# A graph network's start: edges and x transferred before W, packed edges written from another queue, scores chained tile by tile

## The chip, the cores and the metric

The kernel runs on one core of one Trainium2 chip. The metric is the device time of one execution in microseconds (us). A core has five engines that run side by side and meet through semaphores: TensorE (PE in the profile; its weight loads are PEld), VectorE (DVE), ScalarE (ACT), GpSimd (POOL) and SyncE (SP). SP, ACT and POOL can issue DMA transfers, each on a queue of its own (SPq, ACTq, POOLq); the transfers run on 16 DMA engines of the core.

## The reference, cut to what matters

625 nodes with rows x of 1024 values, 20000 edges (`src`, `dst`, a type from 0 to 7). Layer 0 is a graph attention, layer 1 a relational convolution with a gate; each is added to its input and normalised.

```python
h = x @ W                                    # 625 x 1024
al = h @ a_l ; ar = h @ a_r
e = exp(-leaky_relu(al[src] + ar[dst], 0.1)) # one score per edge
rowsum = segment_sum(e, src)
h_prime = segment_sum(e[:, None] * h[dst], src) / (rowsum[:, None] + EPS)
x = layernorm(x + elu(h_prime))
# layer 1
u = x @ root + bias
for r in range(8):                           # mean over the incoming edges of type r
    u = u + mean_r(x) @ weight[r]
z = concat([u, x], 1) @ w_gate + b_gate
x = layernorm(x + tanh(u) * z + x * (1 - z))
```

## The kernel before, in words

The function `fast` does the work. (A second function, `general`, is only entered when the edge counts show that `fast` lost an edge.) Nodes are cut into five tiles of 125 rows.

Layer 0 never gathers rows by edge. It counts how often each pair (source, destination) occurs, by type, and works with dense 625 x 625 matrices:

- *Edges.* The lists dst, src and type are loaded as 125 rows of 160 (L700) into a part of the buffer of `attT`; x's first tile is loaded between the first and the second (L702). These four loads are issued from ACT's queue. W comes in eight chunks of 128 rows from SP's queue (`load_w0`, L567), then x's second tile (L706) and the two halves of `a` (L707, L708). POOL writes two small pads around the DRAM tensor `packed` (L704, L705).
- *Packing.* VectorE converts the lists and packs each edge into one number (L721, L727 to L731). ACT's queue writes the result to `packed` in DRAM (L733). VectorE also compares samples of the sorted list with the first row of each group of destinations (`less`, L723).
- *Groups.* TensorE sums `less` into the place where each group's edges begin (p_count, L737, L738). VectorE turns this into block numbers (L740, L742), and POOL gathers those blocks from `packed` by two indirect DMAs (L746).
- *h's first tile.* `x_turned` transposes x's tile on TensorE (L673) and copies it with ScalarE (L714). `h_parts` multiplies it by W chunk by chunk, two matmuls of 512 columns for each of eight chunks (L779); each float32 matmul shows as two records of the trace. Before the last chunk, `place_edges` turns the gathered edges with TensorE (p_edges, L753) and VectorE splits them into sources and keys (L756 to L764).
- *Counting.* For each of 55 groups VectorE builds one-hot matrices (`one_hots`, L805), and TensorE multiplies them (`counts_of`, L829); ScalarE copies the counts out (L834). In between, TensorE computes the other four tiles of h. `row_sums` (L790) forms al and ar, `all_types` (L842 to L846) adds the types into one count `c` per pair, and the counts go to DRAM for layer 1 (`store_counts`, L881).
- *Scores.* `scores_of(j)` forms the scores `e` of one tile of destinations j against all five tiles of sources (L859 add, L862 multiply by the count cut at 1, L863 leaky relu, L864 exponential on ScalarE, L865 multiply by the count, L866 reduce to `rsum`). `turn_scores(j)` transposes them (patt, L875) and ScalarE copies them to `attT` (L877). `gather_h(t, j)` multiplies them with h (phh, L684).
- *After that.* `attend(t)` divides, applies the elu and normalises (L1058 to L1068), and layer 1's matrix products follow (L1015, L1016, L1019, L1185). Their weights are split on ScalarE and VectorE into three pieces (`prepare`, L988 to L991); the first of these splits, of `root`, lie already beside the scores.

The order of the score work is written with a list `due`: while the groups are counted, a piece of work is done when its group number comes. `AHEAD` tiles of scores are put on that list (L927), the others are computed in the loop of gathers:

```python
        turn_scores(0, es[0])
        for j in range(ST):
            gather_h(0, j)
            if len(es) < ST:
                es.append(scores_of(len(es)))
            if j + 1 < ST:
                turn_scores(j + 1, es[j + 1])
            for t in range(1, EARLY):
                gather_h(t, j)
```

This is the order of the source. A scheduler then fixes the order of the instructions on each engine, and it moves instructions that do not depend on each other past one another. On an engine they run strictly in that fixed order. Each DMA signals its landing on a semaphore; the DMAs of SP and ACT take eight of these in turn, so that a DMA waits until the one eight places before it has landed.

Of the kernel before, what the change touches and what calls it, by code (L numbers as in the profile page):

```python
# [10 lines left out]
F32 = mybir.dt.float32  # L11
F16 = mybir.dt.float16
BF16 = mybir.dt.bfloat16
I32 = mybir.dt.int32
I16 = mybir.dt.int16
AF = mybir.ActivationFunctionType
OP = mybir.AluOpType
# [423 lines left out]
ST = 5  # L441
TN = N // ST
SP = ST * 128
BLOCK = 32
NBLOCK = E // BLOCK
GCOLS = 12
NG = -(-TN // GCOLS)
NGS = ST * NG
# [4 lines left out]
HOTS = 5  # L453
H_GROUPS = 38
LAG = 4
AHEAD = 3
EARLY = 3
MAGIC = 1.5 * 2.0 ** 23
EPS12 = 2.0 ** -12
# [32 lines left out]
def rows_of(t):  # L492
    return TN
# [30 lines left out]
def fast(  # L524
# [16 lines left out]
    nc = tc.nc  # L541
# [13 lines left out]
    def bank(name):  # L555
        return ps[0].tile([128, 512], F32, tag="bank", name=name)


    def load_w0(wpool):

        chunks = []
        for k in range(KC):
            if k % 2:
                w = rawp.tile([128, 2, HALF], F32, tag="raw", name=f"w0_{k}").rearrange("p i c -> p (i c)")
            else:
                w = wpool.tile([128, D], F32, tag="w", name=f"w0_{k}")
            nc.sync.dma_start(w, w0[k * 128:(k + 1) * 128, :])  # L567
            chunks.append(w)
        return chunks
# [18 lines left out]
    ones16 = const.tile([128, 1], F16, name="ones16")  # L588
# [5 lines left out]
    ahead16 = const.tile([1, NGS, 2], F16, name="ahead16")  # L594
    nc.gpsimd.iota(ahead16, pattern=[[0, NGS], [128 // BLOCK, 2]], base=0, channel_multiplier=0,
                   allow_small_or_imprecise_dtypes=True)
    later = const.tile([128, 2, 4], F32, name="later")
# [15 lines left out]
    rsum = const.tile([128, ST, ST], F32, name="rsum")  # L613
# [29 lines left out]
    packed = dram.tile([NBLOCK + 5, BLOCK], F32, name="packed")  # L643
# [4 lines left out]
    def move_rows(n, dma):  # L648

        r0 = 0  # L650
        for m in (n // 16 * 16, n % 16):
            dma(slice(r0, r0 + m))
            r0 += m

    def load_x(pool, t, name, bufs=None, eng=nc.sync, clear=False):

        xt = pool.tile([128, D], F32, tag="x", name=f"{name}_{t}", bufs=bufs)
        if t < ST - 1:
            eng.dma_start(xt, x[t * TN:t * TN + 128, :])
        else:  # L660
            if clear:
                nc.gpsimd.memset(xt[96:], 0.0)
            xr = x[t * TN:t * TN + rows_of(t), :]
            move_rows(rows_of(t), lambda rows: eng.dma_start(xt[rows], xr[rows]))
        return xt
# [22 lines left out]
    with tc.tile_pool(name="f_w", bufs=4, side="right") as wpool, \  # L688
# [7 lines left out]
        per = E // TN  # L696
        edge_rows = free[:TN, D:D + 3 * per].bitcast(I32).rearrange("p (i c) -> p i c", i=3)
        rest, pack, samples = (free[:TN, D + i * per:D + (i + 1) * per] for i in (3, 4, 5))
        for i, ap in ((1, dst), (0, src), (2, etype)):
            nc.scalar.dma_start(edge_rows[:, i, :], ap.rearrange("(p c) -> p c", c=per))  # L700
            if i == 1:
                x_next = load_x(xin, 0, "x", eng=nc.scalar)  # L702
        w0_sb = load_w0(wpool)
        nc.gpsimd.dma_start(packed[0:1, :], pad[:, :BLOCK])  # L704
        nc.gpsimd.dma_start(packed[NBLOCK + 1:, :].rearrange("(o i) c -> o (i c)", o=1), pad)  # L705
        x_next = [x_next, load_x(xin, 1, "x")]  # L706
# [3 lines left out]
        def x_turned(t):  # L710
            n = rows_of(t)
            xt = x_next.pop(0)
            xT = xin.tile([128, KC, 128], F32, tag="xT", name=f"xT_{t}")
            transposed(xt, n, f"px_{t}", lambda ks, p: nc.scalar.copy(xT[:, ks, :n], p))  # L714
            if t + 2 < ST:
                x_next.append(load_x(xin, t + 2, "x"))
            return xT
# [4 lines left out]
        less = scores.tile([TN, per // BLOCK, 2 * NGS], F16, name="less")  # L722
# [7 lines left out]
        nc.vector.scalar_tensor_tensor(pack, edge_rows[:, 1, :], float(LO * TR), pack, op0=OP.mult, op1=OP.add)  # L730
        nc.vector.scalar_tensor_tensor(pack, edge_rows[:, 2, :], float(LO), pack, op0=OP.mult, op1=OP.add)  # L731
        packed_rows = packed[1:NBLOCK + 1, :].rearrange("(p m) c -> p (m c)", p=TN)
        nc.scalar.dma_start(packed_rows, pack)  # L733
        xT_next = x_turned(0)
        p = bank("p_count")
        for m in range(per // BLOCK):
            nc.tensor.matmul(p[:2 * NGS, :1], less[:, m, :], ones16[:TN], start=m == 0, stop=False)  # L737
        nc.tensor.matmul(p[:2 * NGS, :1], ahead16.rearrange("p g h -> p (g h)"), ones16[:1], start=False, stop=True)  # L738
        base = scores.tile([2 * NGS, 1], F32, name="base")
        nc.vector.tensor_copy(base, p[:2 * NGS, :1])  # L740
        at_block = scores.tile([2 * NGS, 2, 4], I32, name="at_block")
        nc.vector.tensor_scalar(at_block, later[:2 * NGS], base, float(NBLOCK + 1), op0=OP.add, op1=OP.min)  # L742
        edges = scores.tile([2 * NGS, 2, 4, BLOCK], F32, name="edges")
        for b in range(2):

            nc.gpsimd.indirect_dma_start(edges[:, b].rearrange("p i c -> p (i c)"), None, packed[:, :],  # L746
                                         bass.IndirectOffsetOnAxis(ap=at_block[:, b, :1], axis=0))

        def place_edges():

            pe = bank("p_edges")[:, :4 * NGS]
            for b in range(2):
                nc.tensor.transpose(pe[:, b * 2 * NGS:(b + 1) * 2 * NGS], edges[:, b].rearrange("p i c -> p (i c)"),  # L753
                                    ident[:2 * NGS, :2 * NGS])
            q = scores.tile([128, 4 * NGS], F32, name="q")
            nc.vector.tensor_scalar(q, pe, 1.0 / LO, 0.5 / LO - 0.5, op0=OP.mult, op1=OP.add)  # L756
            nc.vector.tensor_scalar(q, q, MAGIC, MAGIC, op0=OP.add, op1=OP.subtract)

            def twice(ap):
                return ap.unsqueeze(2).to_broadcast([128, 4 * NGS, 2])  # L760

            nc.vector.tensor_tensor(key2.rearrange("p b g h w -> p (b g h) w"), twice(q),
                                    twice(firsts.rearrange("p b g h -> p (b g h)")), op=OP.subtract)
            nc.vector.scalar_tensor_tensor(src2.rearrange("p b g h w -> p (b g h) w"), twice(q), -float(LO), twice(pe),  # L764
                                           op0=OP.mult, op1=OP.add)
# [8 lines left out]
        def h_parts(t, xT):  # L774
            n = rows_of(t)
            halves_h = [ps_h.tile([128, 512], F32, tag="ph", name=f"ph_{t}_{half}") for half in range(2)]
            for k in range(KC):
                for half, p in enumerate(halves_h):
                    nc.tensor.matmul(p[:n, :], xT[:, k, :n], w0_sb[k][:, half * HALF:(half + 1) * HALF],  # L779
                                     start=k == 0, stop=k == KC - 1)  # L780
                if k == KC - 1:
                    for half, p in enumerate(halves_h):
                        nc.scalar.copy(h_sb[:n, t, half * HALF:(half + 1) * HALF], p[:n, :])
                yield
# [64 lines left out]

        ar_b = attp.tile([128, SP], F32, name="ar_b")  # L850

        def scores_of(j):

            n = rows_of(j)
            cols = slice(j * 128, j * 128 + n)
            c1 = ct[j]
            e = attp.tile([128, ST, 128], F32, name=f"e_{j}")
            e = e[:, :, :n]
            nc.vector.tensor_tensor(e, ar_b[:, cols].unsqueeze(1).to_broadcast([128, ST, n]),  # L859
                                    al.unsqueeze(2).to_broadcast([128, ST, n]), op=OP.add)  # L860

            nc.vector.scalar_tensor_tensor(e, c1, 1.0, e, op0=OP.min, op1=OP.mult)  # L862
            nc.vector.scalar_tensor_tensor(e, e, SLOPE, e, op0=OP.mult, op1=OP.max)  # L863
            nc.scalar.activation(e, e, AF.Exp, scale=-1.0)  # L864
            nc.vector.tensor_tensor(e, e, c1, op=OP.mult)  # L865
            nc.vector.tensor_reduce(rsum[:, :, j], e, axis=AX.X, op=OP.add)  # L866
            return e

        def turn_scores(j, e):
# [11 lines left out]
                nc.sync.dma_start(cd[r][:, :, j * 128:(j + 1) * 128], cj[:, :, r, :])  # L881

        for k, _ in enumerate(h_parts(0, xT_next)):
            if k == KC - 2:
                place_edges()
        due = [(LAG, row_sums, 0)]
# [32 lines left out]
        for i in range(NGS):  # L919
            while steps < min(n_steps, (i + 1) * n_steps // H_GROUPS):  # L920
                next(h_steps, None)
                steps += 1
                if steps % KC == 0:
                    due.append((i + (LAG if steps < n_steps else 0), row_sums, steps // KC))
                    if steps == n_steps:
                        due.append((i + 6, lambda _: spread_ar(), None))
                        due.extend((max(i + 6 + 4 * j, (j + 1) * NG + LAG), lambda _: es.append(scores_of(len(es))), None)  # L927
                                   for j in range(AHEAD))
            if i % NG == 0:
# [20 lines left out]
# [8 lines that stand above are left out]
# [169 lines left out]
    p = bank("p_ins")  # L1127
# [8 lines left out]
    p = bank("p_all")  # L1136
# [22 lines left out]
    for r in range(R):  # L1159
        for h in range(2):  # L1160
# [13 lines left out]
            c = cf[0]  # L1174
# [119 lines left out]
```

## Time and profile before

| | us |
|---|---|
| median of 3 runs (lowest to highest) | 979.65 (977.29 to 980.05) |
| the profiled execution's own time | 980.44 |
| its span, first to last instruction | 978.5 |
| TensorE busy | 945.4 |
| VectorE busy | 595.6 |
| ScalarE busy | 391.3 |
| GpSimd busy | 38.4 |

The profile is of one execution. "Busy" is the time in which an engine ran an instruction; the rest of the span it waited, and the profile says for what, with the line of the kernel. A line such as `PE px L673 <- DMA x<-in_x_dram` reads: TensorE, at the transposes of line 673 that write px, waited for the DMA that writes x. Tables of stretches give for each stretch the busy time of each engine and the number of its instructions, then the clock granted to TensorE (1.00 is full), the busy share of the DMA engines and the bytes they moved.

### The profile page before, as it was taken

Reading aid. Unit: us, or ns where it says so; the run is one execution under the profiler, and the core shown is the slowest. Engines: PE = TensorE matmul, PEld = TensorE weight load, DVE = VectorE, ACT = ScalarE, POOL = GpSimd, SP = SyncE. Lnnn points to the kernel's source line nnn. Section 1 sums busy time; section 2 is a strip of 40 time slices with the busy share of each in tenths; the row PEclk is TensorE's granted clock in tenths of the full one; section 3 lists DMA queues with packets and bytes.
Section 4 is the critical chain, followed back from the end, with each engine's and each line's share of the span. In section 5 each row is a group of like instructions: output and inputs, shape, how many; then the busy total and the mean of one; then the engine's idle time right before and its main releaser. Section 6 shows DMA issues by size and latency. Waiting matters only on the chain.

```text
span 978.5 us, 10845 instructions
## 1 busy us (share of the span) xinstructions
PE 945.4 (97%) x4075; PEld 731.2 (75%) x4075; DVE 595.6 (61%) x955; ACT 391.3 (40%) x714; POOL 38.4 (4%) x68
## 2 busy tenths in 40 slices
PE   3999899999999999999999999999999999999995
PEld 1455554878888888888888888888888888888874
DVE  1697898986536456266365463562653644639995
ACT  0233656344515515425435345244442551433422
POOL 2000001000000000000000000000000000002123
PEclk9999989999999999999999999999999999999998
DMA  7132773533213022122121220320320211432213
GB/s 273 45 76 54 194 203 108 173 117 112 64 34 116 26 65 76 45 86 66 55 86 44 77 87 10 110 65 22 120 65 22 86 37 49 143 114 66 86 43 108
DMA packets 61713, 83.89 MB, mean 86 GB/s; under 512 B 29311, under 2 KB 29833, under 8 KB 61654
## 3 DMA queue, kind: packets, MB, share of 16 engines
q1 hardware_dynamic: 60830, 82.17, 27.1%
q10 hardware_dynamic: 664, 0.84, 0.3%
q8 instruction: 34, 0.56, 0.2%
q14 instruction: 25, 0.20, 0.1%
q0 software_dynamic: 160, 0.11, 0.0%
HBM read 71.36 MB, written 11.75 MB: 85 GB/s over the span
## 4 chain that ended last, share of the span: by engine, by line
PE 94%; DVE 2%; DMA 1%; ACT 1%; issue 0%; POOL 0%; ACTq 0%; POOLq 0%; DVEq 0%
PE pu L1185 19%; PE p_w L1015 15%; PE p_w L1016 15%; PE p_w L1019 15%; PE ph L779 7%; PE phh L684 5%; PE p_root L1019 2%; PE p_root L1015 2%; PE p_wgx L1019 2%; PE p_wgx L1016 2%; PE p_wgx L1015 2%; PE p_root L1016 2%; PE pc L829 2%; DMA attT<-in_edge_type_dram 1%; PE p_wgu L1019 1%; PE p_wgu L1016 1%
## 5 line engine op out<-in xcount | busy, mean ns | idle before, releaser
L1016 PE MATMUL p_w<-m_w,x_l 128*128 128x512 f32 x640 | 249.1, 389 | 0.0
L1015 PE MATMUL p_w<-g_w,x_h 128*128 128x512 f32 x640 | 249.0, 389 | 0.0
L1185 PE MATMUL pu<-y,cf 125*128 125x512 f32 x800 | 184.4, 389 | 0.0
L1167 DVE SCALAR_TENSOR_TENSOR v<-p_w,v 125x512 f32<-125x512 f32 x80 | 55.2, 690 | 201.8 <-PE p_w L1019 153.0
L1019 PE MATMUL p_w<-e_w,x_d 128*128 128x512 f32 x640 | 176.4, 389 | 0.0
L1185 PEld LDWEIGHTS pu<-y,cf 125*128 125x128 f32 x800 | 150.2, 188 | 31.5
L1019 PEld LDWEIGHTS p_w<-e_w,x_d 128*128 128x128 f32 x640 | 120.2, 188 | 25.5 <-DVE e_w L991 0.3
L1016 PEld LDWEIGHTS p_w<-m_w,x_l 128*128 128x128 f32 x640 | 120.2, 188 | 25.1 <-DVE m_w L990 0.2
L1015 PEld LDWEIGHTS p_w<-g_w,x_h 128*128 128x128 f32 x640 | 120.2, 188 | 25.0
L1166 ACT ACTIVATE v<-p_w 125x512 f32<-125x512 f32 x80 | 47.6, 596 | 214.0 <-PE p_w L1016 214.0
L990 DVE SCALAR_TENSOR_TENSOR m_w<-raw_w,e_w 128x512 fp32r<-128x512 f32 x128 | 84.7, 682 | 36.4 <-ACT e_w L989 36.4
L1170 DVE TENSOR_TENSOR y<-v,y 125x512 fp32r<-125x512 f32 x80 | 55.2, 690 | 50.8 <-ACT y L1169 50.8
L988 ACT ACTIVATE g_w<-raw_w 128x512 fp32r<-128x512 f32 x128 | 73.2, 621 | 29.8 <-PE p_w L1015 20.7
L991 DVE TENSOR_TENSOR e_w<-g_w,m_w 128x512 fp32r<-128x512 f32 x128 | 84.7, 682 | 0.5
L1169 ACT CAST y<-v 125x512 fp32r<-125x512 f32 x80 | 49.2, 615 | 75.1 <-DVE v L1167 75.1
L779 PE MATMUL ph<-w,xT 128*125 128x512 f32 x160 | 77.7, 614 | 1.1 <-ACT xT L714 1.1
L989 ACT ACTIVATE e_w<-raw_w 128x512 fp32r<-128x512 f32 x128 | 73.2, 623 | 0.0
L1189 DVE SCALAR_TENSOR_TENSOR L_gnn_bias_dram_u<-pu,inv,L_gnn_bias_dram_u 125x512 f32<-125x512 f32 x80 | 55.4, 740 | 0.5
L1151 ACT CAST cf<-cs 128x640 fp32r<-128x640 f16 x40 | 25.9, 724 | 54.7 <-PE pu L1185 46.1
L779 PEld LDWEIGHTS ph<-w,xT 128*125 128x125 f32 x160 | 27.9, 192 | 25.0 <-issue 22.3
L1232 POOL TENSOR_TENSOR L_gnn_bias_dram_u<-L_gnn_bias_dram_u,xr 125x512 f32<-125x512 f32 x10 | 17.0, 1697 | 744.5 <-ACT L_gnn_bias_dram_u L1217 711.9
L684 PE MATMUL phh<-h_sb,attT 125*125 125x512 f32 x100 | 45.8, 613 | 0.2 <-ACT attT L877 0.2
(156 smaller groups left out, 969.5 us busy)
## 6 DMA issues: line engine op xcount, KB each, us to landing
raw_w<-in_L_gnn_weight_dram SPq DMA_DIRECT2D x64, 512.0 KB
cd<-cj SPq DMA_DIRECT2D x40, 160.0 KB
cs<-cd SPq DMA_DIRECT2D x8, 800.0 KB
w<-in_L_gnn_W_dram SPq DMA_DIRECT2D x8, 512.0 KB
raw_root<-in_L_gnn_root_dram SPq DMA_DIRECT2D x8, 512.0 KB
raw_wgx<-in_L_gnn_w_gate_dram SPq DMA_DIRECT2D x8, 512.0 KB
raw_wgu<-in_L_gnn_w_gate_dram SPq DMA_DIRECT2D x8, 512.0 KB
x<-in_x_dram SPq DMA_DIRECT2D x7, 512.0 KB
```

The lines of the kernel that those rows point to most:

```text
L684: nc.tensor.matmul(banks_h[t, half][:n, :], attT[:nj, j, tile_cols(t)], h_sb[:nj, j, half * HALF:(half + 1) * HALF], start=(j == 0), stop= ...
L779: nc.tensor.matmul(p[:n, :], xT[:, k, :n], w0_sb[k][:, half * HALF:(half + 1) * HALF], start=k == 0, stop=k == KC - 1)
L988: nc.scalar.activation(g, w, AF.Copy, scale=DOWN)
L989: nc.scalar.activation(e, w, AF.Copy, scale=UP12 * DOWN)
L990: nc.vector.scalar_tensor_tensor(m, w, UP12, e.bitcast(F32), op0=OP.mult, op1=OP.subtract)
L991: nc.vector.tensor_tensor(e, g.bitcast(F32), m.bitcast(F32), op=OP.subtract)
L1015: nc.tensor.matmul(p1, h[:, k, :], g, start=k == 0, stop=False, skip_group_check=True)
L1016: nc.tensor.matmul(p1, l[:, k, :], m, start=False, stop=k == KC - 1, skip_group_check=True)
L1019: nc.tensor.matmul(p2, d[:, k, :], e, start=k == 0, stop=k == KC - 1, skip_group_check=True)
L1167: nc.vector.scalar_tensor_tensor(v[:n], p2, -EPS12, v[:n], op0=OP.mult, op1=OP.add)
L1185: nc.tensor.matmul(p, c[:m, t, j * 128:(j + 1) * 128], piece[:m], start=(t == 0 and i == 0), stop=(t == ST - 1 and i == 1), skip_group_che ...
L1189: nc.vector.scalar_tensor_tensor(at, p[:n], inv[:n, j, r:r + 1], at, op0=OP.mult, op1=OP.add)
```

## The change

Four edits. The three edge lists and x's first tile are loaded from SP's queue, ahead of W, and no longer from ACT's. The packed edges are written from POOL's queue. The group counts with what follows them, up to the gathers, become a function that is called after the first step of h's first tile. The scores of a tile depend on the sum of the tile before: the scalar 1.0 of the multiply is read from a column of a new tile `turn`, which VectorE computes as min(rsum, 0) + 1 from the last tile's `rsum` (a sum of exponentials times counts, never negative, so the value is always 1). And `AHEAD` goes from 3 to 1.

```diff
-AHEAD = 3
+AHEAD = 1
...
         for i, ap in ((1, dst), (0, src), (2, etype)):
-            nc.scalar.dma_start(edge_rows[:, i, :], ap.rearrange("(p c) -> p c", c=per))
+            nc.sync.dma_start(edge_rows[:, i, :], ap.rearrange("(p c) -> p c", c=per))
             if i == 1:
-                x_next = load_x(xin, 0, "x", eng=nc.scalar)
+                x_next = load_x(xin, 0, "x")
...
-        nc.scalar.dma_start(packed_rows, pack)
+        nc.gpsimd.dma_start(packed_rows, pack)
         xT_next = x_turned(0)
-        p = bank("p_count")
...
+        def gather_edges():
+
+            p = bank("p_count")
...
+            return edges
...
+        turn = attp.tile([128, ST], F32, name="turn")
+        nc.vector.memset(turn[:, :1], 1.0)
...
-            nc.vector.scalar_tensor_tensor(e, c1, 1.0, e, op0=OP.min, op1=OP.mult)
+            nc.vector.scalar_tensor_tensor(e, c1, turn[:, j:j + 1], e, op0=OP.min, op1=OP.mult)
...
             nc.vector.tensor_reduce(rsum[:, :, j], e, axis=AX.X, op=OP.add)
+            if j + 1 < ST:
+                nc.vector.tensor_scalar(turn[:, j + 1:j + 2], rsum[:, 0, j:j + 1], 0.0, 1.0, op0=OP.min, op1=OP.add)
             return e
...
         for k, _ in enumerate(h_parts(0, xT_next)):
+            if k == 0:
+                edges = gather_edges()
             if k == KC - 2:
                 place_edges()
```

The body of `gather_edges` is what stood in line before (L735 to L747), unchanged.

More of the change, by code (lines that the diff above doesn't have):

```diff
@@ L732, in fast @@
         packed_rows = packed[1:NBLOCK + 1, :].rearrange("(p m) c -> p (m c)", p=TN)
-        nc.scalar.dma_start(packed_rows, pack)
+        nc.gpsimd.dma_start(packed_rows, pack)
         xT_next = x_turned(0)
-        p = bank("p_count")
[L736 to L747, printed above, removed]
+        def gather_edges():
+            p = bank("p_count")
+            for m in range(per // BLOCK):
+                nc.tensor.matmul(p[:2 * NGS, :1], less[:, m, :], ones16[:TN], start=m == 0, stop=False)
+            nc.tensor.matmul(p[:2 * NGS, :1], ahead16.rearrange("p g h -> p (g h)"), ones16[:1], start=False, stop=True)
+            base = scores.tile([2 * NGS, 1], F32, name="base")
+            nc.vector.tensor_copy(base, p[:2 * NGS, :1])
+            at_block = scores.tile([2 * NGS, 2, 4], I32, name="at_block")
+            nc.vector.tensor_scalar(at_block, later[:2 * NGS], base, float(NBLOCK + 1), op0=OP.add, op1=OP.min)
+            edges = scores.tile([2 * NGS, 2, 4, BLOCK], F32, name="edges")
+            for b in range(2):
+                nc.gpsimd.indirect_dma_start(edges[:, b].rearrange("p i c -> p (i c)"), None, packed[:, :],
+                                             bass.IndirectOffsetOnAxis(ap=at_block[:, b, :1], axis=0))
+            return edges
         def place_edges():
```

## The prediction

> **What bounds the kernel now.** I read the engine shares first, then who TensorE (PE) waits for, then the chain that ended last, then the stretches around TensorE's waits.
>
> ```profile
> PE 945.4 (97%) x4075; PEld 731.2 (75%) x4075; DVE 595.6 (61%) x955; ACT 391.3 (40%) x714; POOL 38.4 (4%) x68
> ```
>
> ```profile
> PE px L673 <- DMA x<-in_x_dram: 8.1, 1, 8.1
> PE p_count L737 <- DVE less L723: 7.4, 1, 7.4
> PE patt L875 <- DVE e L865: 2.8, 1, 2.8
> PE p_wgu L1019 <- DVE e_wgu L991: 1.6, 2, 1.0
> ```
>
> TensorE is busy 97% of the span, and nearly all it ever waits (us in total, times, longest) stands before 19 us, with one wait of 2.8 us at the first scores. The change touches just these two places, so what it does to TensorE there is passed on to the end. The chain in order of time (start, us):
>
> ```profile
> 2.10 14.22 DMA attT<-in_edge_type_dram
> 16.41 0.34 DVE attT L731
> 16.77 0.27 ACTq L733
> 17.07 1.28 ACT L714
> 18.36 0.59 ACT xT L714
> 18.99 14.08 PE ph L779 x28
> ```
>
> h begins at 18.99 not because of W but because the third edge list, sharing with W the DMA engines (96 to 104% busy from 3 to 11 us), reaches VectorE (DVE) at 16.41. L733, in front of x's copies on ScalarE (ACT), waits for it, and ScalarE then still loads its function table (1.28). The counts (p_count) wait for the same list.
>
> The second place is the scores, by stretches (us; PE, PEld, DVE, ACT, POOL busy; clock; DMA share, GB/s):
>
> ```profile
> 120.00:122.00 2.00, 0.00 (x0) 0.00 (x0) 2.00 (x4) 2.00 (x5) 0.00 (x0) 0.91 1.05 215
> 122.00:124.00 2.00, 1.47 (x6) 1.21 (x6) 2.00 (x4) 1.38 (x4) 0.00 (x0) 0.50 0.67 139
> 126.00:128.00 2.00, 2.00 (x5) 0.96 (x5) 2.00 (x3) 0.22 (x1) 0.00 (x0) 0.50 1.04 215
> 128.00:130.00 2.00, 2.00 (x8) 1.26 (x8) 2.00 (x4) 1.64 (x4) 0.36 (x1) 0.88 0.57 116
> ```
>
> TensorE stands still from 119.6 to 122.3, its clock then halves for some 6.8 us, and VectorE is full.
>
> **The compiled order.** TensorE's instructions stand in the same order as before but for one matmul of the gathers that changes places. The counts, though written after h's first step, still stand between x's turns and h's first matmul: that part of the change does nothing on TensorE. ScalarE loses its five DMAs; SyncE (SP) has four more, ahead of W; GpSimd (POOL) issues the packed write between its pads and its memsets. VectorE's order changes only in the scores.
>
> **1. Start of h.** Ahead of W now stand 512 KB of x and three lists of 78.1 KB. For a first landing with little beside it the nearest row is the gathers' 2.7 to 3.0 us: 0.73 + 2.7 = 3.4 for dst. x at the 0.38 MB/us of the stretches from 3 to 11 us: 1.35, so 4.8. One list costs 0.2 us at that rate, and 3.6 us beside W (src seen at 12.77, the type list at 16.41); I take 1.0, nearer the low end, as nothing runs beside it: src 5.8, types 6.8. VectorE: L727 to L730 take 1.2, L731 0.3, less 0.7 (rows at 12.77 to 17.4): 8.0. Counts 0.8 (17.43 to 18.23): 8.8. Beside it x's turns (1.9) and copies (1.1) end by 7.8, the table load at the very start, and W's first chunk (512 KB, 1.35) by 8.2. So h starts at about 9.0: **-10.0**, between 8.2 and 13 (each list at 2.3). W's chunks follow every 1.35 us; TensorE takes 1.72 for each (four records of 0.43): W is never late.
>
> [...]
>
> **2. Its clock.** The first weight loads of h follow each other every 0.85 us until 22.6, then every 0.43: 3.6 us at half speed, 1.8 lost. The other slow stretch lasted 6.8 us. So the new start loses 1.7 to 3.4; I take 2.3: **+0.5** (-0.1 to +1.6).
>
> [...]
>
> **3. The packed edges.** They are ready at L731's end, 7.3. GpSimd has finished its pads by 5.9; the write is queued before its memsets (0.39 and 0.48) and the gathers, nothing else. No trace shows a 78 KB write from GpSimd. Low: the gathers' 3.0 us to landing. High: the same write on ScalarE's queue, 16.77 to 23.92, 7.15 us, plus the pads' 5.7. I take 7, near the ACT row: 14.3 (10.3 to 20.2). The gathers then take 4.4 (23.92, second at 25.34, 3.0 to land), with traffic up to 7.1: edges at 18.7 (14.7 to 27.3). TensorE asks for them 13.9 us after h's start (18.99 to 32.91), and 0.5 for the clock: 23.4. Covered; the cover ends at 23.4 and each us beyond costs one, 4 at most: **+0.3**.
>
> From there to the last count (111 to 120 us before) TensorE was busy 97.2 of 97.5 us; order and durations stay, all shifts alike. x's later tiles and a's rows come behind W on SP's queue, by some 20 us, before their use at 24 and later.
>
> **4. Scores in sequence.** Before, VectorE ran two tiles side by side (0.72 from operation to operation). Now tile j+1's L862 waits for tile j's reduce over `turn` (about 0.1, row of the small operations L960 to L963), and the compiled order fills the holes with the splits of root (L990/L991, 0.60 each). In the times of before:
> - Tile 0 is ready a little earlier, its L865 at 121.1 for 121.4: TensorE resumes at 122.0 for 122.3.
> - Tile 1's L865: from 121.1 VectorE runs L865 (0.72), L842 of the last tile (1.39), the reduce (0.72), L844 (0.73), turn (0.1), an add (0.72), L846 (0.41), tile 1's multiply (0.72), an add (0.72) and L863 (0.8): 128.1. The exponential (0.73) stands on ScalarE behind nine splits (0.52 each) that follow tile 0's copies, and starts at 128.7: L865 at 129.5.
> - Each later tile: L865 0.72, split 0.60, reduce 0.72, split 0.60, turn 0.1, split 0.60, multiply 0.72, split 0.60, L863 0.72, two splits 1.2 (beside the exponential of 0.73): 6.6 us. TensorE's own work per tile is 0.54 + 12 x 0.43 = 5.7. VectorE is the bound.
> - Tile 4: 129.5 + 3 x 6.6 = 149.3; its turn 0.95 later at 150.3, where before it was 145.05: **+5.2**.
>
> Running these orders with these durations by hand gives 145.2 for before, 0.1 off the trace. The slow clock matters little now: if it lasted from 121.6 to 138.7, TensorE would end the stage 1.7 later; with none, 0.2 earlier. So 5.0 to 6.9. Does anything later take it back? From 146 to 173 TensorE was busy 27.0 of 27.0, and x1's first tile, normalised at 159.8, waited for TensorE until 162.8: no. Root's second half is loaded in another order but still some 20 us before its use.
>
> **Sum**: -10.0 + 0.5 + 0.3 + 5.2 = -4.0. The profiled execution took 980.44 (span 978.5 and 1.9 around it): 976.4. It lies 0.8 above the median of the three runs (979.65); I take half of that off: **976.0**.
>
> **Rivals.**
> - *The clock halves at every gap* (slower). The gaps before tiles 1 to 4 (3.2, then three of 0.9) could keep TensorE at half speed: 11.4 us a tile against 6.6, three times 4.8, 14.4 in all: 990. It decides against the change once it costs over 4. For: 2.8 us of waiting was enough in before. Against: at half speed TensorE fills the gaps, and busy it recovered within 6.8 us.
>   [...]
> - *The edges or lists are late.* Lists at 2.3 us (h at 13) or edges at 27.3 cost 4: 980, no change. For: three lists took 16 us in before, and pads 5.7. Against: W ran beside them.
> - *The sequence is hidden.* If the gathers of the stage were late for another reason, item 4 is free: 980.44 - 9.2, 971. Against it: no wait of TensorE after 124 in before.
> - *The counts do sit inside h's first tile*, as written: h need not wait for 8.8 but for W's chunk at 8.2: 0.8 better, 975. The compiled order speaks against it.
>
> **Chances.** Forecast 0.55 (974 to 978.5), lists or edges late 0.22 (978.5 to 982.5), sequence hidden or counts moved 0.14 (970 to 974), clock 0.09. A measurement of this kernel tells about 0.3%, 2.9 us, from no change: under 976.7 is faster, which takes 0.41 of the forecast's 0.55 and the 0.14: 0.55; within, 0.14 and 0.22: 0.36; slower 0.09. The range, 971.5 to 982, leaves out most of the clock case and the edge of the hidden one; the forecast's own range is 974 to 978.5.
>
> **What would show it.** h's first matmul at 8.2 to 10 right behind the counts; ScalarE's table load near 1 us; no wait of TensorE on the edges at 23; TensorE waiting for L865 of `e` five times, 2.5, 3.2 and three times 0.9; `turn` on VectorE's chain; tile 4's turn some 28 us after tile 0's, for 22.7. Wrong would be: h waiting for W, a wait at the edges, or TensorE continuous through the scores.

## The result, and the profile after

| | before | changed |
|---|---|---|
| median (lowest to highest), us | 980.05 (977.29 to 980.77), 5 runs | 974.81 (973.86 to 975.51), 5 runs |
| the profiled execution, us | 980.44 | 973.86 |
| its span, us | 978.5 | 972.1 |
| h's first matmul at | 18.99 | 8.57 |
| edges asked for (p_edges) at | 32.91 | 22.35 |
| e's tile 0 turned (patt) at | 122.34 | 111.51 |
| e's tile 4 turned at | 145.05 | 139.58 |
| layer 1's first turn of x (px) at | 162.76 | 157.36 |

The changed kernel is faster by 0.5%: the ratio is 0.995, 95% interval 0.9933 to 0.9966. The profiled execution of the changed kernel is the fastest of its five. The rows below the span are from TensorE's instructions in order of time, one profiled execution each.

The engine shares of the changed kernel hardly differ from those of before; only the waits do.

```profile
PE 945.3 (97%) x4075; PEld 730.5 (75%) x4075; DVE 597.2 (61%) x960; ACT 391.4 (40%) x714; POOL 39.5 (4%) x69
```

TensorE's waits in the changed kernel (us in total, times, longest):

```profile
PE patt L883 <- DVE e L871: 7.6, 3, 4.9
PE px L673 <- POOL firsts L605: 4.7, 1, 4.7
PE p_count L739 <- DVE less L723: 1.2, 1, 1.2
```

At the start 8.1 and 7.4 us became 4.7 and 1.2. (The first is put down to GpSimd; in e3 and e8, which load in the same order, it is put down to the DMA of x, at 4.60 and 4.62.) At the scores 2.8 us became 7.6. The two places move against each other, and but for 1.0 us late in the profiled executions that is the whole result.

The chain of the changed kernel's start (start, us, what):

```profile
1.59 3.93 DMA attT<-in_src_dram
...
6.82 0.32 DVE attT L731
7.14 0.65 DVE less L723
...
7.84 0.62 PE p_count L739 x5
8.46 0.17 PE p_count L740
8.64 13.87 PE ph L782 x28
```

ScalarE is gone from this chain, and the wait for a list ends at 5.5 us instead of 16.4. The counts still stand ahead of h's first matmul, as the compiled order said.

The scores of the changed kernel by stretches (busy us of PE, PEld, DVE, ACT, POOL; clock; DMA share, GB/s):

```profile
111.00:113.00 2.00, 1.09 (x6) 0.92 (x7) 2.00 (x3) 2.00 (x6) 0.00 (x0) 1.00 0.94 194
...
115.00:117.00 2.00, 0.00 (x0) 0.00 (x0) 2.00 (x4) 2.00 (x5) 0.00 (x0) 1.00 1.04 215
117.00:119.00 2.00, 0.00 (x0) 0.00 (x0) 2.00 (x4) 1.97 (x5) 0.36 (x1) 0.69 0.52 107
...
121.00:123.00 2.00, 2.00 (x3) 0.77 (x3) 2.00 (x5) 0.84 (x3) 0.00 (x0) 0.50 1.06 254
```

VectorE is full in every stretch. TensorE turns tile 0 at full clock and stands still from 114.7 to 119.6. The clock halves within that wait, at about 117.8, and is full again at about 124.6.

The chain that ended last shows which engine sets the pace. From tile 0's turn to the last tile's it was TensorE's own work before, but for one copy on ScalarE:

```profile
139.52 0.54 PE patt L875 x5
140.06 5.15 PE phh L684 x12
145.21 0.54 PE patt L875 x5
```

and it is VectorE's in the changed kernel:

```profile
131.99 0.72 DVE e L871
...
138.71 0.73 DVE e L871
139.58 0.78 PE patt L883 x5
```

### The profile page after: what moved, and what is told of

The parts are those of the page before. It is cut to its first block, busy times and chain, and to the rows that moved or that the text cites. A ratio compares the mean times of both kernels' runs of the same rounds, so it can differ in the third digit from the quotient of the medians.

```text
span 972.1 us, 10853 instructions
## 1 busy us (share of the span) xinstructions
PE 945.3 (97%) x4075; PEld 730.5 (75%) x4075; DVE 597.2 (61%) x960; ACT 391.4 (40%) x714; POOL 39.5 (4%) x69
## 4 chain that ended last, share of the span: by engine, by line
PE 92%; DVE 5%; ACT 1%; DMA 1%; SPq 0%; issue 0%; POOL 0%; POOLq 0%; DVEq 0%; ACTq 0%
PE pu L1195 19%; PE p_w L1026 15%; PE p_w L1025 15%; PE p_w L1029 15%; PE ph L782 7%; PE phh L684 3%; PE p_root L1029 2%; PE p_root L1025 2%; PE p_wgx L1029 2%; PE p_wgx L1026 2%; PE p_wgx L1025 2%; PE p_root L1026 2%; PE pc L832 2%; PE p_wgu L1029 1%; PE p_wgu L1026 1%; PE p_wgu L1025 1%
```

## The experiments

The theory: the start's edits give all of the gain, because lists and x no longer share the DMA engines with W; `turn` costs some 5 us of it, because VectorE then works on one tile after another. The rivals: the gain is that of the freed ScalarE queue; the loss is that of `AHEAD`; the loss is that of the half clock.

All runs in one table. Medians are of 4 to 12 runs; the rest is from each kernel's profiled execution, in us. "First tile" runs from h's first matmul to the edges' transposes (in e7, e11 and e12 it has the counts in it, 0.4 to 0.7 us), "scores" from the turn of e's tile 0 to layer 1's first turn of x, "half clock" is the time at 0.50 within the scores or the gap before them, read from stretches of 0.5 us.

| kernel | median | h at | first tile | tile 0 to tile 4 | scores | half clock |
|---|---|---|---|---|---|---|
| before | 980.05 | 18.99 | 13.92 | 22.71 | 40.42 | 6.8 |
| changed | 974.81 | 8.57 | 13.78 | 28.07 | 45.85 | 6.8 |
| e1 start alone | 969.73 | 10.31 | 15.14 | 21.44 | 39.16 | 3.4 |
| e2 scores alone | 986.06 | 19.27 | 14.27 | 28.07 | 45.86 | 13.7 |
| e3 turn, AHEAD 3 | 975.49 | 8.62 | 14.73 | 27.54 | 45.28 | 13.7 |
| e4 AHEAD 1, no turn | 973.01 | 8.51 | 14.57 | 25.60 | 43.31 | 3.4 + 3.4 |
| e5 write on ACT | 977.53 | 10.38 | 15.03 | 28.33 | 46.04 | 3.4 + 6.8 |
| e6 write alone | 980.18 | 19.68 | 14.69 | 21.37 | 39.09 | 3.4 |
| e7 counts inside | 969.23 | 8.40 | 15.02 | 22.86 | 40.57 | 6.8 |
| e8 warm | 966.97 | 8.42 | 14.71 | 20.08 | 37.80 | 0 |
| e9 behind W | 977.77 | 18.78 | 13.81 | 20.08 | 37.79 | 0 |
| e10 changed, warm | 972.06 | 9.20 | 13.71 | 27.16 | 42.37 | 0 |
| e11 warm, counts inside | 967.49 | 8.42 | 14.60 | 20.08 | 37.79 | 0 |
| e12 warm from the start | 966.05 | 9.11 | 12.62 | 20.08 | 37.80 | 0 |

Before was run beside each group of four: medians 980.83 (e1 to e4), 980.01 (e5 to e8) and 980.74 (e9 to e12). A difference of medians between groups can be off by as much as these differ, 0.8 us; where it matters, the difference by the ratios to before is given too.

### e1: the start alone

```diff
 # from the changed kernel
-AHEAD = 1
+AHEAD = 3
...
-        turn = attp.tile([128, ST], F32, name="turn")
-        nc.vector.memset(turn[:, :1], 1.0)
...
-            nc.vector.scalar_tensor_tensor(e, c1, turn[:, j:j + 1], e, op0=OP.min, op1=OP.mult)
+            nc.vector.scalar_tensor_tensor(e, c1, 1.0, e, op0=OP.min, op1=OP.mult)
...
-            if j + 1 < ST:
-                nc.vector.tensor_scalar(turn[:, j + 1:j + 2], rsum[:, 0, j:j + 1], 0.0, 1.0, op0=OP.min, op1=OP.add)
```

> The change without its part in the scores (AHEAD is 3 again, there is no turn); it computes the same. Theory (the start gives 10.4 us, the dependence through turn takes 5.1 of them, nothing else counts): h begins at about 8.6 us, the transposes of e's tile 0 at about 111.8, of tile 4 at about 134.5 (before's times less 10.5), and the time is 974.8 - 5.1, about 969.5 us. Rival that the sequence costs nothing because something later sets the end: 974 to 975 us. Rival that the start's gain is given back by the weights' loads once nothing else delays TensorE: the first p_root stays near 167 us and the time near 974.

Measured: 969.73 (968.78 to 971.20), ratio to before 0.9891 (0.9872 to 0.9910). The start alone gives 980.83 - 969.73 = 11.1 us; the score edits take 974.81 - 969.73 = 5.1 of it (5.8 by the ratios, 0.995 and 0.9891). Both rivals by which the time would stay at 974 are out.

The profiled execution, the highest of its five, also shows something that the changed kernel's did not: VectorE waited for the type list (VectorE's instructions in order of time; start, us, what, the idle time before it in brackets).

```profile
8.56 0.32 DVE L731 SCALAR_TENSOR_TENSOR attT<-attT 125x160 f32<-125x160 int32 x1 [1.77 <-DMA attT<-in_edge_type_dram]
```

The list, issued at 1.95 us in both, came 1.7 us or more later here. It is last ahead of W, and W's chunks run beside its end, which may be the reason but was not tried; `less` and h come 1.74 us later with it.

### e2: the scores alone

```diff
 # from the kernel before
-AHEAD = 3
+AHEAD = 1
...
+        turn = attp.tile([128, ST], F32, name="turn")
+        nc.vector.memset(turn[:, :1], 1.0)
...
-            nc.vector.scalar_tensor_tensor(e, c1, 1.0, e, op0=OP.min, op1=OP.mult)
+            nc.vector.scalar_tensor_tensor(e, c1, turn[:, j:j + 1], e, op0=OP.min, op1=OP.mult)
...
+            if j + 1 < ST:
+                nc.vector.tensor_scalar(turn[:, j + 1:j + 2], rsum[:, 0, j:j + 1], 0.0, 1.0, op0=OP.min, op1=OP.add)
```

> The kernel before with AHEAD at 1 and turn added; its start is that of before; it computes the same. Theory: h at about 19.0 us as before, e's tile 0 transposed at about 122.2, its tile 4 at about 150.2 (28 us after tile 0, before 22.7), the time 980.05 + 5.2, about 985 us, with a 95% interval of the ratio above 1. Rival (the sequence is hidden behind the gathers): 980 us. Rival (the slow clock is what costs, at each tile's gap): beyond 988 us, with a granted clock near 0.5 at more than one tile.

Measured: 986.06 (985.08 to 986.36), ratio 1.0056 (1.0039 to 1.0073): 5.2 us slower. The tiles span 28.07 us, to the digit those of the changed kernel, though the half clock lasted twice as long, 13.7 us for 6.8. It covered both tile 0 and tile 1, as the clock's rival had it, but the time beyond 988 did not come with it.

### e3 and e4: turn and AHEAD one by one

```diff
 # e3, from the changed kernel
-AHEAD = 1
+AHEAD = 3
```

> The changed kernel with AHEAD at 3 again and turn kept: the scores still depend on one another from tile to tile, but VectorE's first three tiles stand in the order of before; it computes the same. Theory (turn costs, AHEAD doesn't): tile 4 of e transposed 28 us after tile 0, the time that of the changed kernel within 0.5 us, 974.3 to 975.3. Rival (the loss of 5 us comes from AHEAD at 1, since fewer tiles stand ready): about 970 us.

```diff
 # e4, from e1
-AHEAD = 3
+AHEAD = 1
```

> The changed kernel without turn, AHEAD left at 1; it computes the same. Theory: without the dependence two tiles of VectorE and ScalarE run side by side, tile 4 of e is transposed some 23 to 24 us after tile 0, and the time is 0 to 1 us above that of the start's edits alone, about 970 us. Rival (AHEAD at 1 carries the loss): 974 to 975 us, tile 4 some 28 us after tile 0.

Measured: e3 975.49 (973.66 to 976.49), ratio 0.9946 (0.9928 to 0.9963), the changed kernel's time, with the tiles 27.54 us apart; e4 973.01 (971.21 to 974.11), ratio 0.9923 (0.9906 to 0.9941), 3.3 above e1 where 0 to 1 was expected. So `turn` alone costs 975.49 - 969.73 = 5.8, `AHEAD` alone 3.3, and both together 5.1. They don't add up: both delay tile 1, and with `turn` the later tiles are late whatever `AHEAD` is. That `AHEAD` costs nothing holds only beside `turn`.

Why e4 cost more than I had reckoned is in the table. TensorE needs 37.80 us for the scores when nothing stops it (e8). In e4 it waited 2.26 us more before tile 1, and the half clock came twice, 112.5 to 115.9 and 119.3 to 122.7: 43.31 - 37.80 - 2.26 = 3.25 us, for 6.8 us at half speed. The expectation had left the second slow stretch out.

### e5, e6 and e9: which edit of the start

```diff
 # e5, from the changed kernel
-        nc.gpsimd.dma_start(packed_rows, pack)
+        nc.scalar.dma_start(packed_rows, pack)
 # e6, from the kernel before
-        nc.scalar.dma_start(packed_rows, pack)
+        nc.gpsimd.dma_start(packed_rows, pack)
 # e9, from e1
+        w0_sb = load_w0(wpool)
         for i, ap in ((1, dst), (0, src), (2, etype)):
...
-        w0_sb = load_w0(wpool)
```

> The changed kernel with the write of the packed edges back on ScalarE's queue; the lists and x's first tile stay on SyncE's, ahead of W; it computes the same. In ScalarE's order the write stands ahead of its table load and of the copies of x's turned tile, so ScalarE stands until pack is written (about 7.2 us). Theory (the order ahead of W is nearly all of the start's gain, the freed ScalarE a little of it): copies from about 8.8 us, h at 9.4 to 9.8 us, the time 0.8 to 1.2 us above the changed kernel's, about 975.8. Rival (the freed queue of ScalarE is what saved the time): h at 15 us or later, 981 us or more.

> The kernel before with only the write of the packed edges moved to GpSimd's queue; lists and x stay on ScalarE's queue; it computes the same. Theory (lists and x arrive late because W's chunks run beside them): less is still made at about 17 us, h waits for the counts, begins at about 18.2 instead of 19.0 us, and the time is 0.7 us below that of before, about 980. Rival (the freed ScalarE is what counts): h begins by 11 us and the time is below 974.

> The start's edits alone (AHEAD 3, no turn), but W's eight chunks stand ahead of the lists and of x's first tile on SyncE's queue; ScalarE's queue is as free as in the changed kernel; it computes the same. Theory (the order ahead of W is the gain): x and the lists land behind W's 4 MB, x's turns begin near 13 to 15 us, h near 17 to 19 us as in before, and the time is 8 us or more above that of the start's edits alone, 978 to 981 us. Rival (the queue or the freed ScalarE is the gain): 970 to 972 us.

Measured: e9 977.77 (976.45 to 980.81), ratio 0.998 (0.9969 to 0.9990), 8.0 us above e1 with the same queues and as free a ScalarE. The chain of e9:

```profile
1.21 4.58 DMA w<-in_L_gnn_W_dram
...
5.80 10.46 DMA x<-in_x_dram
...
16.40 1.90 PE px L673 x8
```

x stands behind W's chunks, its turns begin at 16.4 and h at 18.78, as late as in before: the order ahead of W is the start's gain, and the queue without that order brings h 0.2 us. Yet e9 lies 3.0 us below its before (980.74). Most of that goes with TensorE's clock. Six of the twelve executions of e9 had a mean granted clock of 0.996, and these took 976.45 to 978.04; of the 17 executions of before beside them one had it, and the eight of before in all groups that had it took 976.27 to 977.67, about the same. Why e9 lost the clock less often is not shown.

e6: 980.18 (979.40 to 981.54), ratio 1.0010 (0.9999 to 1.0020), no change; the rival, below 974, is out. In its chain TensorE has lost ScalarE as its last releaser and waits for the list itself:

```profile
2.10 15.74 DMA attT<-in_edge_type_dram
...
18.95 0.62 PE p_count L737 x5
```

Still h began at 19.68 in the profiled execution and not at the 18.2 expected: VectorE had the type list at 17.93, 1.5 us later than in before. Beside W the list's landing varies by more than the 0.7 us to be won.

e5: 977.53 (976.66 to 978.37), ratio 0.9976 (0.9965 to 0.9987), 2.7 above the changed kernel where 0.8 to 1.2 was expected, and below the rival's 981. Its chain:

```profile
7.54 0.33 DVE attT L731
...
7.90 0.52 ACTq L733
...
8.45 1.28 ACT L714
...
9.75 0.59 ACT xT L714
```

The mechanism is the one expected: the write, the table load and the copies stand in a row. Its size was short. VectorE's L728 took 0.94 us for 0.24 in the changed kernel, and h began 1.81 us after the changed kernel's. The first tile then took 15.03 us for 13.78, but that lies within the 13.71 to 15.14 of the kernels with the same loads and is not put down to the write. The longer L728 is a side of the write that I hadn't seen. In the changed kernel it stands on GpSimd's queue ahead of GpSimd's memsets and waits there for pack, and they run from 7.98 to 8.76, after VectorE's chain (done at 7.78). Without it they ran from 5.91 to 6.69, and L728, begun at 5.85, ended at 6.79. One execution shows it; it was not tried apart. So moving the write is worth some 1.8 us at h's start and up to 2.7 in all once the lists are early, and nothing that can be measured while they are late (e6).

### e7: the counts really inside h's first tile

```diff
 # from e1; the counts are held behind the last matmul of h's first step
-                edges = gather_edges()
+                with tc.issue_after(getattr(last_h[0], "ins", last_h[0])):
+                    edges = gather_edges()
```

> The start's edits alone (AHEAD 3, no turn), and the counts really held behind the first two products of h on TensorE; it computes the same. Theory: h no longer waits for less, so neither for the type list, which came late in the profiled run of the start's edits alone (less at 8.80 us, h at 10.31): h begins at 7.6 to 8.2 us with W's first chunk, and the time is 0.5 to 2 us below that of the start's edits alone, 968 to 969 us. Rival (the place of the counts doesn't matter): 969.7 us.

Measured: 969.23 (966.88 to 970.20), ratio 0.9889 (0.9871 to 0.9907); 0.5 below e1, with overlapping runs. TensorE's new wait names the reason:

```profile
PE ph L784 <- DMA w<-in_L_gnn_W_dram: 1.9, 1, 1.9
```

h begins at 8.40 with W's first chunk, where the counts in the changed kernel were done by 8.6: no more than 0.2 us to win when the type list is in time. The medians can't tell the theory's small gain from the rival's none.

### e8, e10, e11 and e12: the clock

```diff
 # e8, from e1; e11, from e7
+        p_warm = bank("p_warm")
+        for m in range(10):
+            nc.tensor.matmul(p_warm, iota16[:, :128], iota16[:, :512], start=m == 0, stop=m == 9)
         begin.close()
 # e10, from the changed kernel, in turn_scores
                 p = bank(f"patt_{j}_{t0}")
+                for m in range((8, 14)[j] if j < 2 and t0 == 0 else 0):
+                    nc.tensor.matmul(p, iota16[:, :128], iota16[:, :512], start=True, stop=True)
 # e12, from e11: 16 products ahead of x's turns, 8 behind them
+        def keep_warm(name, times):
+            p = bank(name)
+            for m in range(times):
+                nc.tensor.matmul(p[:, :256], ones.bitcast(F16)[:, :128], ones.bitcast(F16), start=True, stop=True)
+        keep_warm("p_warm_x", 16)
         xT_next = x_turned(0)
+        keep_warm("p_warm_h", 8)
```

> The start's edits alone (AHEAD 3, no turn), and 10 products of 128x512 that nothing reads, on TensorE between the last counts and the transposes of e's first tile, in a gap of 2.8 us; what is stored is the same. Theory (without turn TensorE sets the pace here, and each gap costs its length and the half clock that follows): the granted clock stays 1.0 from 112 to 170 us, the transposes of tiles 0 to 4 span 19.8 us plus nothing (start's edits alone: 21.4, before: 22.7), and the time is 1.7 us or more below that of the start's edits alone, 966.5 to 968 us. Rival (the half clock is hidden): 969.7 us. If the 10 products run over the gap, the first transposes move back by some tenths of a us.

> The changed kernel, turn and AHEAD 1 included, with 8 products that nothing reads in TensorE's gap before e's tile 0 and 14 before its tile 1; what is stored is the same. Theory (VectorE's chain of 6.6 us a tile sets the pace with turn, so the clock hardly counts): the granted clock stays near 1.0, tile 4 is still transposed about 28 us after tile 0, TensorE waits for e at each tile instead, and the time stays within 1 us of the changed kernel's, 973.8 to 975. Rival (the loss of 5 us is the clock's, since the gaps and the clock lost while TensorE was busy add up to it as well): tile 4 at 25 us after tile 0 and 972 us or less.

> The start's edits alone with the counts held behind h's first two products and with the 10 products in the gap before e's tile 0; what is stored is the same. If the place of the counts is worth nothing when the type list is in time, 967 us as with the 10 products alone; if it is worth the wait for the list, 966 to 966.5.

> As the kernel with the counts inside and 10 products before e's tile 0, and 24 products of 128x256 that nothing reads on TensorE before h, 16 ahead of x's turns and 8 behind them; what is stored is the same. Theory (h's first 3 to 5 us run at half clock since TensorE stood idle before): h's first tile takes 12.0 to 12.5 us to the edges' transposes and no 13.9 to 15, unless W's chunks or the edges are late, and the time is 1.5 to 2.4 us lower, about 965 us. Rival (W's chunks at 1.35 us or the edges at 22 us set the pace of the first tile): no gain, 967 us, with waits of ph for W or of p_edges for the edges.

e8: 966.97 (966.83 to 967.94), ratio 0.9873 (0.9856 to 0.9891), 2.8 below e1 (1.8 by the ratios). TensorE's instructions of e8:

```profile
109.62 2.32 PE L953 MATMUL p_warm<-iota 128*128 128x512 f16 x10
112.55 0.78 PE L879 MATMUL patt<-ident,e 125*125 125x125 f32 x5 [0.61 <-DVE e L869]
115.55 0.71 PE L879 MATMUL patt<-ident,e 125*125 125x125 f32 x5
```

The ten products fill 2.3 of the 2.8 us, the clock stays full, and the tiles span 20.08 us (19.8 expected). Without `turn`, the half clock is a real cost.

e10: 972.06 (971.69 to 973.17), ratio 0.9918 (0.9904 to 0.9931), 2.75 below the changed kernel (3.1 by the ratios). The theory allowed 1 and its time was missed; 972 was the rival's time. But the rival's reason, tile 4 at 25 us after tile 0, is not what came: it was 27.16. VectorE's last product of e for tiles 0 and 4, first in the changed kernel:

```profile
110.56 0.80 DVE L871 TENSOR_TENSOR e<-e,c 128x625 f32<-128x625 f32 x1
...
138.63 0.80 DVE L871 TENSOR_TENSOR e<-e,c 128x625 f32<-128x625 f32 x1
```

and in e10, at full clock throughout:

```profile
111.12 0.81 DVE L871 TENSOR_TENSOR e<-e,c 128x625 f32<-128x625 f32 x1
...
139.20 0.80 DVE L871 TENSOR_TENSOR e<-e,c 128x625 f32<-128x625 f32 x1
```

28.07 and 28.08 us: the clock does nothing to VectorE's chain, which sets when tile 4 is ready. The gain stands behind tile 4. The compiled order of e10 puts one more pair of gathers ahead of each of tiles 2, 3 and 4, so that fewer are left (changed kernel, then e10):

```profile
140.19 17.33 PE L684 MATMUL phh<-h_sb,attT 125*125 125x512 f32 x40
```

```profile
140.76 14.76 PE L684 MATMUL phh<-h_sb,attT 125*125 125x512 f32 x34
```

That is 17.33 - 14.76 = 2.57 of the 2.75 us. By an estimate from these rows TensorE needs the full clock for it (14 records of 0.43 and the turn of 0.54 fill the 6.6 us of a tile); whether part of it could be had at the half clock was not tried, since order and clock changed together here. With the clock full on both sides the chained scores still cost 4.6 us: 42.37 in e10 for 37.80 in e8. So most of their cost is not the clock's.

e11: 967.49 (966.91 to 967.74), ratio 0.9869 (0.9853 to 0.9886): with the clock held, the place of the counts is worth nothing that can be measured.

e12: 966.05 (965.24 to 966.95), ratio 0.9854 (0.9837 to 0.9872), the fastest here, 1.4 below e11. h's first tile took 12.62 us with the counts in it: all of it at the full pace of 0.43 us a record. It gave less than the 14.60 - 12.62 = 2.0 us, as W's first chunk came 0.7 later. The chain shows that the next bound is reached:

```profile
15.86 6.24 DMA edges<-packed,at_block
...
22.14 0.31 PE p_edges L763
```

The edges land at 22.1, just when TensorE wants them.

## Why the prediction was right, step by step

The mechanism held: the start gives about 10 us, the chained scores take about 5, and nothing later takes anything back or hides it.

- **Start of h, -10.0.** -10.42 (18.99 to 8.57). The terms held as well: dst seen at 3.38 (3.4 taken), x's turns at 4.71 (4.8), src at 5.54 (5.8), `less` done 0.2 early, counts 0.8. The value of 1.0 for a list, in place of up to 3.6, fits the profiled execution: src was seen 0.83 us after x, and the type list at most 1.28 after src. In e1 that last step took 3.0, so the choice near the low end was partly luck.
- **Its clock, +0.5.** -0.14 in the profiled execution (first tile 13.78 for 13.92). Over the changed kernel, e1, e3, e4, e5, e8 and e10, which share the start's loads and have the counts ahead of h, the first tile took 13.71 to 15.14, 14.52 in the mean: +0.6 over the one execution of before that the prediction had. With e2, e6 and e9, whose loads are late, before's mean is 14.17, and +0.35 is left. The length differs from execution to execution, so the -0.14 is luck, and +0.5 was near the middle. The loss of 2.3 us in it was an estimate; against the tile's 28 records of 0.43 us (12.0) these seven kernels took 1.7 to 3.1 longer. The half speed is read from the pace of h's records here; the granted clock of the profile reads 1.00 throughout the first tile.
- **Edges, +0.3.** No wait, as taken for the likely case, but this was the worst-sized step. The write was issued at 7.44 and let the gathers go at 13.63, where 14.3 was taken; the second gather started at 15.05, and the median gather took 6.5 us from issue to landing, where I had 3.0 from a row of before. That makes 21.6 in place of 18.7, asked for at 22.35: a cover of 0.8 us, not 4.7. In before the gathers had DMA engines that were 18 to 77% busy (stretches from 24 to 28 us); now W and what follows it keep them 99 to 104% busy from 13 to 21. e12 used the cover up.
- **Scores, +5.2.** Tile 4 was turned 28.07 us after tile 0, 22.71 before. Measured against tile 0's own shift that is +5.4, and against the start's, +5.1, as tile 0 came 0.26 sooner (0.3 taken). VectorE's period was 6.60 in the changed kernel (118.70, 125.30, 131.90), as added up by hand. The waits came otherwise: three, of 2.5, 4.9 and 0.2, and not five, since the half clock fell on the gathers of tile 1 instead of tile 0's; it filled the gaps of 0.9 that were expected. e10 shows that VectorE's chain is the same with and without it. The prediction also had the stage end only 0.2 earlier with no slow clock; e10 gained 2.75, but in another order of the gathers, so this was not tried as it was meant.
- **Sum.** -4.0 was forecast and -6.6 measured in the two profiled executions. Of the difference, 1.0 lies behind 157 us, in work that the change doesn't touch: from layer 1's first turn of x to the end of the span takes 815.7 in before, 814.7 in the changed kernel, and also 814.7 in e6, which is before in all but one write. Up to that turn it was -5.4 (162.76 to 157.36); 0.4 of the excess over -4.0 is the start's, 0.6 the first tile's clock, 0.3 the wait for the edges that didn't come. Between the medians it was -5.2. I had taken off half of the profiled execution's distance to the median (0.4), which was in the right direction.

The rivals. The clock did not halve at every gap of the changed kernel; in e4 and e5 it did halve twice, and that cost e4 some 3.3 us, while e5's scores took only 0.2 more than the changed kernel's, as VectorE sets the pace there. The lists were late by 1.7 us in e1's profiled execution and by 0.5 to 0.6 in e10's and e12's, and not by 4. The sequence was not hidden (e1). The counts don't stand inside h's first tile, and it makes no difference that can be measured (e7, e11). What the prediction left unsaid is that `AHEAD` has a price of its own, 3.3 us, which `turn` covers.

## What to carry to other kernels

Small loads that the first work needs belong ahead of the large ones: three lists and one tile of 0.75 MB ahead of 4 MB brought the start forward by 10 us, while the same loads on a queue of their own beside W (before, e6) or behind it (e9) left it near 19 us. A dependence between iterations is paid where the engine that runs them is near its limit: write down that engine's operations for one round (here 6.6 us) and compare them with the bound engine's work for the same round (5.7). And where the bound engine stands (here TensorE, for 2.77 us before tile 0, with 0 to 6.8 us at half clock in the five kernels that had that wait), price the slow clock behind the wait too (e8 is 2.8 us below e1), on a kernel in which that engine is the bound after the wait.

## What the runs showed of the hardware

- The same wait of 2.77 us before tile 0 was followed by no half clock (e9), by 3.4 us of it (e1, e6) or by 6.8 us (before, e7). The scores then took 37.8, 39.1 to 39.2 and 40.4 to 40.6 us: some 1.3 to 1.4 us for each 3.4. The single stretches at half clock in the table last 3.4, 6.8 or 13.7 us, the longer ones about two and four times the shortest. In before the clock dropped some 2.1 us into that wait, in e1 some 0.5 us behind its end. What starts such a stretch and what sets its length, no run here shows.
- With ten products that nothing reads, 2.3 us in a gap of 2.8, the clock stayed full in the profiled executions of e8, e11 and e12; without them, after the wait of 2.77, it did so in one of five. With 3.4 us of such products before x's turns and 1.0 behind them, h's first tile ran at its full pace from the start (e12).
- The granted clock of the profile does not show the slow pace at the changed kernel's start: h's weight loads come every 0.85 us until about 12.0 us and every 0.43 from there on, while the granted clock reads 1.00 in every stretch of 0.5 us from 0 to 30.
- VectorE's L728 took 0.94 us in e5, where GpSimd's memsets ran beside it (5.91 to 6.69), and 0.24 in the changed kernel and in before, where they did not. In e5 it began at 5.85, 0.06 ahead of the memsets by the profile, whose spans on GpSimd are rough, and ended at 6.79, 0.1 behind them. It is one execution, and no run here shows the cause.
- A gather of 110 rows from GpSimd's queue took 2.7 to 3.0 us to land in before, with DMA engines 18 to 77% busy, and 6.3 to 6.7 in the changed kernel, with full ones (99 to 104%).
